# An encoder-decoder block on one core: the two decoder parts under one order, block 0's cross attention among the second batch's units, feed-forward weights loaded in the tail

## The chip, the cores and the metric

The kernel runs on one core of a Trainium2 chip. The metric is the device time of one execution in microseconds (us), as the median of several timed runs. One further execution was recorded by the hardware profiler; all views of the profile come from it. The engines are named as the profile does: PE (TensorE, matmuls and transposes) with PEld (its weight loads), DVE (VectorE), ACT (ScalarE), POOL (GpSimd) and SP (SyncE, which issues the DMAs here). Each engine works through its own instructions in order.

## The reference

Everything is float32, with D = 512, 16 heads of 32, a feed-forward width of 2048, and two batches. The context (2 x 77 x 512) goes through one encoder layer; the target x (2 x 2048 x 512) through one decoder layer that attends to it:

```python
x = src                                              # context, 77 rows per batch
x = x + _mha(_ln(x), _ln(x), enc..., bias=eb)        # encoder self attention
x = x + relu(_ln(x) @ enc_ff1_w.T) @ enc_ff2_w.T
memory = x
y = tgt                                              # 2048 rows per batch
y = y + _mha(yn, yn, dec_sa..., bias=sb)             # yn = _ln(y); sb: relative bias, causal
y = y + _mha(_ln(y), memory, dec_ca..., bias=cb)     # cross attention over 77 keys
y = y + relu(_ln(y) @ dec_ff1_w.T) @ dec_ff2_w.T
```

(Biases and the norms' scales and shifts are left out here; the kernel has them.) The relative bias depends on the distance of key and query, clamped at 127.

## The kernel before

Each batch of 2048 rows is cut into four blocks of 512 (`NMB`), each block into four tiles of 128 rows (`TB`): eight blocks in all, numbered 0 to 7. Every name with a small t is a tile of a block.

**Part one: self attention (and the encoder).** A unit is one tile of 128 queries and one group of four heads: 16 units to a block, 128 in all, and units 64 to 127 are the second batch. A loop over the units writes the order out by hand. For unit n it issues `slot(n)`, and then for each piece of up to four blocks of keys: `turn` (TensorE transposes the probabilities, L365, and DVE or ACT copies them to `pts`, L369 and L371), scores of a later unit (`scores`, L321, with the maximum and copy to `pp` on DVE, L330 and L337, and the exponential on ACT, L345), and `values` (L384). Even units keep their probabilities at the low end of the big buffer `pp`, odd units at the high end, each in four times (block + 1) x 512 columns. `slot(n)` runs what is listed for that unit: `light[n]` (short steps: norms of the next block, the division by the softmax sums in two steps, residual rows, loads of the bias) and then `jobs[n]` (a projection each of queries, keys, values or the output: 4 matmuls of 128x512, L185, L196, L207, L219). A job's weights are loaded two jobs ahead. The encoder is cut into stages, which stand in `light` of the first units; its results, keys and values for the cross attention, go to DRAM (`ckT_d`, `cv_d`). After the last unit, 16 more slots hold the rest: the last division in the first two of them, the output projections of block 7 (L219) seven to ten slots after the last unit. Self attention's results go to DRAM as `y1`, row tile by row tile.

**Part two: cross attention and feed-forward.** It has its own pools of SBUF and PSUM, which take the place of part one's. All its weights are loaded at its beginning (`w_1` and `w_2`, the feed-forward's, with 4 MB each). A block's cross attention (`cross_slots`) is laid over 32 slots: the norm of each tile in three stages (statistics; centering on DVE, L809, with the next bias row added by POOL, L810; transposes, L814, copied by ACT, L819, and DVE, L821), queries (L893), then per tile scores (L833; DVE adds the bias for the first two tiles of a batch, L841, takes the maximum, L843, and subtracts it, L844), exponential, sums and division (POOL, L852), transposes (L860), values (L872), output (L881), and the next norm. A block's feed-forward (`forward_slots`) has 16 first-layer groups (L924) and 16 second-layer quarters (L930), one per slot. The main loop runs block n's feed-forward and block n + 1's cross attention side by side, slot by slot. Block 0's cross attention has no feed-forward beside it and stands alone ahead of the loop:

```python
nT3 = late()
for _ in cross_slots(*steps[0], ys_of[0], nT3):
    pass
for n, (b, m) in enumerate(steps):
    ...
    for _ in range(SLOTS):
        next(side, None)
        next(feed)
```

SyncE issues every DMA in the order in which the program writes it, and waits in that order. In PSUM, part one has seven rotating banks and one (`ot`) for the values' sums; part two has six rotating and two for the feed-forward.

Of the kernel before, what the change touches and what calls it, by code (L numbers as in the profile page):

```python
# [17 lines left out]
P = 128  # L18
# [36 lines left out]
def tile_encoder_decoder(ctx: ExitStack, tc: tile.TileContext, ins, out):  # L55
# [82 lines left out]

    y1 = [
        [dram.tile([P, TB, D], F32, name=f"y1_{b}_{m}", tag=f"y1_{b}_{m}") for m in range(NMB)]  # L140
        for b in range(B)
    ]
    with (
# [10 lines left out]
        END = 2 * HC * T  # L154
        bv = bcast_row(ac, "sa_bv")
        bo = bcast_row(ac, "dec_sa_out_b")
        def bank():
            return ps.tile([P, 512], F32, name="s", tag="s", bufs=7)
# [8 lines left out]
        def small_w(c0):  # L167
            w = sb.tile([P, NC, P], F32, name="wqk", tag="wqk", bufs=3)
            nc.sync.dma_start(w, wchunk("dec_sa_in_wT", c0, P))
            return w  # L170

        def big_w(kind, b, m):
            if wbig.get("is") != (kind, b, m):
                w = sb.tile([P, NC, D], F32, name="wbig", tag="wbig")
                nc.sync.dma_start(
                    w, wchunk("dec_sa_in_wT", 2 * D) if kind == "v" else wchunk("dec_sa_out_wT", 0)
                )
                wbig["is"], wbig["w"] = (kind, b, m), w
            return wbig["w"]
# [73 lines left out]
        def norm_turn(b, m, t):  # L253
            xn = xs.pop((b, m, t))
            if t == 0:
                nTs[b, m] = sb.tile([P, NC, MB], F32, name="nT", tag="nT")
# [94 lines left out]
        def turn(n, j):  # L351
# [9 lines left out]
            for o, group in enumerate(order):  # L361
                pt = bank()
                pts = sb.tile([P, HC, P], F32, name="pts", tag="pts", bufs=6)
# [10 lines left out]
        def values(n, j):  # L374
            b, m, g, t = units[n]
            k0, kn = parts[n][j]
            if t == 0 and j == 0:
                state["ot"] = ps.tile([P, TB, P], F32, name="ot", tag="ot", bufs=1)
# [9 lines left out]
            if t == TB - 1 and j == len(parts[n]) - 1:  # L388
                o = sb.tile([P, TB * P], F32, name="oT", tag="oT", bufs=6)
                nc.scalar.copy(o, ot)  # L390
                ots[b, m, g] = o
# [276 lines left out]

        blocks = [(b, m) for b in range(B) for m in range(NMB)]
# [4 lines left out]
        for x, (b, m) in enumerate(blocks):  # L674
# [14 lines left out]
            for t in range(TB):  # L689
                jobs[u + NU + 7 + t].append(out_job(b, m, t))  # L690
                light[u + NU + 6 + t].append(lambda b=b, m=m, t=t: residual(b, m, t))
# [49 lines left out]

        slot(-1)
# [20 lines left out]
        for n in range(end, end + NU):  # L763
            slot(n)

    with (
        tc.tile_pool(name="bw", bufs=1) as bw,
        tc.tile_pool(name="bsb", bufs=1) as sb,
        tc.tile_pool(name="bsm", bufs=5) as sm,
        tc.tile_pool(name="bps", bufs=1, space=PSUM) as ps,
        tc.manual_schedule(),
    ):
        w_q = bw.tile([P, NC, D], F32, name="w_q")
        w_o = bw.tile([P, NC, D], F32, name="w_o")
        w_1 = bw.tile([P, NC, DFF], F32, name="w_1")  # L780
        w_2 = bw.tile([P, NF, D], F32, name="w_2")
        ckT = bw.tile([P, NC, B * S], F32, name="ckT")
        cv = bw.tile([S, B, D], F32, name="cv")

        cb = [bw.tile([P, H, S], F32, name=f"cb{i}") for i in range(2)]
        SLOTS = NF + TB * NC

        def bank():
            return ps.tile([P, 512], F32, name="s", tag="s", bufs=6)

        def new_y(b, m):
            ys = [sb.tile([P, D], F32, name="y", tag="y", bufs=12) for _ in range(TB)]
            for t, y in enumerate(ys):
                nc.sync.dma_start(y, y1[b][m][:, t, :])
            return ys

        def norm_stages(ys, t, n, row, nT):

            y = ys[t]
            st = sm.tile([P, 6], F32, name="bnst", tag="bnst")  # L800
            mv = sm.tile([P, 2], F32, name="bnmv", tag="bnmv")
            rs = sm.tile([P, 2], F32, name="rstd", tag="rstd")
            nc.vector.bn_stats(st, y)
            nc.vector.bn_aggr(mv, st)
            nc.vector.tensor_scalar_add(rs[:, 0:1], mv[:, 1:2], EPS)
            nc.gpsimd.tensor_tensor(rs[:, 1:2], rs[:, 0:1], mhalf[:, 0:1], ALU.pow)
            yield
            xn = sb.tile([P, D], F32, name="xn", tag="xn", bufs=2)
            nc.vector.tensor_scalar(xn, y, mv[:, 0:1], rs[:, 1:2], ALU.subtract, ALU.mult)  # L809
            nc.gpsimd.tensor_tensor(y, y, row, ALU.add)  # L810
            yield
            pt = bank()
            for c in range(NC):
                nc.tensor.transpose(pt[:, ts(c, P)], xn[:, ts(c, P)], ident)  # L814
            for c in range(NC):
                d = nT()[:, c, ts(t, P)]
                sc, bi = vec(f"dec_{n}_s", c), vec(f"dec_{n}_b", c)
                if c % 2:
                    nc.scalar.activation(d, pt[:, ts(c, P)], AF.Identity, bias=bi, scale=sc)  # L819
                else:  # L820
                    nc.vector.tensor_scalar(d, pt[:, ts(c, P)], sc, bi, ALU.mult, ALU.add)  # L821
            yield

        def attend_stages(b, i, q, y):

            kT, v = ckT[:, :, ts(b, S)], cv[:, b, :]
            pr = sb.tile([P, HC, NC, S], F32, name="pr", tag="pr", bufs=2)
            mx = sm.tile([P, HC, NC], F32, name="mx4", tag="mx4", bufs=3)
            banks = [bank() for _ in range(HC)]
            for g in range(NC):  # L830
                for r in range(HC):
                    rows = slice(r * HD, (r + 1) * HD)
                    nc.tensor.matmul(  # L833
                        banks[r][:, ts(g, S)], q[rows, g, :], kT[rows, g, :], start=True, stop=True
                    )
            for r in range(HC):
                s = banks[r][:, : NC * S].rearrange("p (g k) -> p g k", k=S)
                d = pr[:, r]
                if i < 2:
                    bias = cb[i].rearrange("p (g r) k -> p r g k", r=HC)[:, r]  # L840
                    nc.vector.tensor_tensor(d, s, bias, ALU.add)  # L841
                    s = d
                nc.vector.tensor_reduce(mx[:, r], s, AX.X, ALU.max)  # L843
                nc.vector.tensor_tensor(d, s, mx[:, r, :, None].to_broadcast([P, NC, S]), ALU.subtract)  # L844
            yield
            nc.scalar.activation(pr, pr, AF.Exp)
            yield
            su = sm.tile([P, HC, NC], F32, name="su4", tag="su4", bufs=2)
            ri = sm.tile([P, HC, NC], F32, name="ri4", tag="ri4", bufs=2)
            nc.vector.tensor_reduce(su, pr, AX.X, ALU.add)  # L850
            nc.vector.reciprocal(ri, su)
            nc.gpsimd.tensor_tensor(pr, pr, ri[:, :, :, None].to_broadcast([P, HC, NC, S]), ALU.mult)  # L852
            yield
            yield
            yield
            turned = []
            for g in range(NC):
                pt = bank()
                for r in range(HC):
# [152 lines left out]
```

## Time and profile before

| | us |
|---|---|
| median of 3 runs (lowest, highest) | 3176.05 (3172.75, 3176.2) |
| the profiled execution | 3170.97 |
| its span, from the first to the last instruction | 3169.1 |
| PE busy | 3054.7 (96%) |
| PE weight loads busy | 1732.0 (55%) |
| DVE busy | 1678.5 (53%) |
| ACT busy | 1300.1 (41%) |
| POOL busy | 258.0 (8%) |
| mean granted clock of PE | 0.986 |

A float32 matmul is recorded as two instructions, a transpose as one. In the lists of groups and in timelines, a row gives the start, the length, the engine, the line of the kernel, the operation, the tiles (out<-in), the shape and the count; in brackets stands how long the engine had been idle before and who ended that. Rows of stretches give, for each, the length, each engine's busy time with its instruction count, the granted clock of PE as a share, the busy share of the DMA engines and GB/s. A matmul's end is modelled, so that rows of one line overlap a little.

### The profile page before, as it was taken

What the parts mean: (1) busy time and instruction counts of PE and PEld (TensorE: products, weight loads), DVE (VectorE), ACT (ScalarE), POOL (GpSimd) and SP (SyncE); (2) the same over time, 40 slices, a digit from 0 to 9 for tenths busy, and PEclk for the clock granted to TensorE, in tenths of its full rate; (3) what the DMA queues carried; (4) which work ended last, traced back from release to release, by engine and by line L of the source; (5) the groups of instructions that cost most, each with busy time, mean ns of one, the idle gap of its engine ahead of it and who ended that gap; (6) DMA issues with size and microseconds to landing.
All of it is one profiled execution on the core that took longest, in us unless ns stands there. A gap on an engine that the chain in (4) does not pass through costs nothing. (4 is left out here: it accounts for less than half of the span.)

```text
span 3169.1 us, 56403 instructions
## 1 busy us (share of the span) xinstructions
PE 3054.7 (96%) x22792; PEld 1732.0 (55%) x22792; DVE 1678.5 (53%) x5347; ACT 1300.1 (41%) x2299; POOL 258.0 (8%) x241
## 2 busy tenths in 40 slices
PE   7899999999999999999999858999999999999999
PEld 4565566666665555666666624545454544454544
DVE  4765667666765777676666535434343434343410
ACT  3443466667775555666677702111111111111100
POOL 0100000000000000000000012111111111111100
PEclk9899999999999999999999978999999999999999
DMA  6413201101111312111011070000000000000000
GB/s 154 106 43 117 79 21 48 55 21 38 31 35 58 84 48 62 50 31 35 18 31 48 2 223 1 4 24 4 24 4 24 4 24 4 24 4 10 4 10 13
DMA packets 103860, 128.42 MB, mean 41 GB/s; under 512 B 12058, under 2 KB 62794, under 8 KB 103090
## 3 DMA queue, kind: packets, MB, share of 16 engines
q1 hardware_dynamic: 103602, 124.83, 13.6%
q8 instruction: 181, 2.97, 0.4%
q14 instruction: 77, 0.63, 0.1%
HBM read 105.03 MB, written 19.77 MB: 39 GB/s over the span
## 5 line engine op out<-in xcount | busy, mean ns | idle before, releaser
L330 DVE TENSOR_SCALAR_CACHE_REDUCE pp<-s 128x512 f32<-128x512 f32 (+3 forms) x1024 | 560.7, 590 | 291.9 <-PE s L321 291.9
L345 ACT ACTIVATE pp<-pp,nm 128x128 f32<-128x128 f32 (+15 forms) x512 | 610.6, 1194 | 151.3 <-DVE nm L344 148.5
L371 ACT COPY pts<-s 128x512 f32<-128x512 f32 (+3 forms) x816 | 408.6, 581 | 413.6 <-PE s L365 412.4
L365 PE MATMUL s<-ident,pp 128*128 128x128 f32 x4352 | 544.2, 276 | 13.8 <-ACT pp L345 10.7
L365 PEld LDWEIGHTS s<-ident,pp 128*128 128x128 f32 x4352 | 481.1, 142 | 119.0 <-issue 98.3
L924 PE MATMUL ff<-nT,w 128*128 128x512 f32 x1024 | 457.3, 596 | 0.5 <-DVE nT L821 0.5
L930 PE MATMUL ff<-w,hT 128*128 128x512 f32 x1024 | 454.9, 594 | 0.0
L321 PE MATMUL s<-kT,q 32*128 32x512 f32 (+3 forms) x2560 | 378.9, 575 | 2.3 <-ACT kT L197 0.8
L384 PE MATMUL ot<-pts,vv 128*32 128x128 f32 x8704 | 341.5, 279 | 28.8 <-DVE pts L369 26.5
L384 PEld LDWEIGHTS ot<-pts,vv 128*32 128x32 f32 x8704 | 219.6, 109 | 266.9 <-issue 142.0
L924 PEld LDWEIGHTS ff<-nT,w 128*128 128x128 f32 x1024 | 190.7, 191 | 221.8 <-issue 219.2
L930 PEld LDWEIGHTS ff<-w,hT 128*128 128x128 f32 x1024 | 189.6, 190 | 215.9 <-issue 214.8
L337 DVE CUSTOM_DVE_ANT_0 pp<-s,bias 128x256 f32<-128x256 f32 (+1 forms) x512 | 210.0, 410 | 63.0 <-PE s L321 63.0
L126 ACT ACTIVATE hT<-ff,vecs 128x512 f32<-128x512 f32 x64 | 44.0, 687 | 431.9 <-PE ff L924 431.8
L369 DVE COPY pts<-s 128x512 f32<-128x512 f32 (+3 forms) x328 | 195.6, 644 | 46.7 <-PE s L365 44.9
L321 PEld LDWEIGHTS s<-kT,q 32*128 32x128 f32 x2560 | 135.7, 183 | 76.3 <-issue 47.1
L819 ACT ACTIVATE nT<-s,vecs 128x128 f32<-128x128 f32 x128 | 58.5, 457 | 242.7 <-DVE nT L821 216.7
L865 ACT COPY pts<-s 77x512 f32<-77x512 f32 x64 | 37.2, 581 | 279.3 <-PE s L860 279.3
L821 DVE TENSOR_SCALAR nT<-s,vecs 128x128 f32<-128x128 f32 x128 | 52.4, 409 | 169.8 <-PE s L814 135.9
L128 DVE TENSOR_SCALAR hT<-ff,vecs 128x512 f32<-128x512 f32 x64 | 48.1, 751 | 152.5 <-PE ff L924 152.5
L185 PE MATMUL s<-nT,wqk 128*128 128x512 f32 x256 | 122.9, 625 | 0.5 <-DVE nT L267 0.5
L881 PE MATMUL s<-w_o,oT 128*128 128x512 f32 x256 | 120.5, 615 | 0.7 <-ACT oT L877 0.7
(111 smaller groups left out, 2628.8 us busy)
## 6 DMA issues: line engine op xcount, KB each, us to landing
wqk<-in_dec_sa_in_wT_dram SPq DMA_DIRECT2D x64, 256.0 KB, 3.7
bias<-tz SPq DMA_DIRECT2D x128, 128.0 KB, 3.5
wbig<-in_dec_sa_in_wT_dram SPq DMA_DIRECT2D x8, 1024.0 KB, 8.0
vv<-in_enc_ff_wT_dram SPq DMA_DIRECT2D x8, 1024.0 KB, 5.8
wbig<-in_dec_sa_out_wT_dram SPq DMA_DIRECT2D x8, 1024.0 KB, 7.8
xr<-in_x_dram SPq DMA_DIRECT2D x32, 256.0 KB, 7.4
y<-xr SPq DMA_DIRECT2D x32, 256.0 KB, 2.5
y<-y SPq DMA_DIRECT2D x32, 256.0 KB, 4.4
```

The costliest lines, as they stand in the source:

```text
L185: nc.tensor.matmul(mm, w[:, c, :], nTs[b, m][:, c, :], start=(c == 0), stop=(c == NC - 1))
L321: nc.tensor.matmul(banks[r][:, : kn * P], q[rows4(r), ts(t, P)], kT[rows4(r), g, k0 * P : (k0 + kn) * P], start=True, stop=True,)
L330: nc.vector.tensor_scalar(p[:, k0 * P : (k0 + far) * P], s[:, : far * P], 1.0, None, ALU.mult, ALU.max, accum_out=st["mx"][:, r, c : c + 1],)
L337: nc.vector.tensor_tensor_reduce(p[:, (i + 1) * P - w : (i + 1) * P], s[:, far * P : kn * P], biases[b, m, g][:, r, 2 * P - w :], 1.0, LOW ...
L345: nc.scalar.activation(p[:, : (i + 1) * P], p[:, : (i + 1) * P], AF.Exp, bias=nm, accum_out=sums_of[b, m, g][:, t, r : r + 1],)
L365: nc.tensor.transpose(pt[:, ts(x, P)], p[r][:, ts(k0 + k, P)], ident)
L369: nc.vector.tensor_copy(pts[:, : len(group), :], pt[:, :w])
L371: nc.scalar.copy(pts[:, : len(group), :], pt[:, :w])
L384: nc.tensor.matmul(ot[rows4(r), t, :], vv[:, k0 + k, ts(g * HC + r, HD)], got[r, k], start=(k0 + k == 0), stop=(k0 + k == nb - 1),)
L881: nc.tensor.matmul(mm, oT[:, ts(c, P)], w_o[:, c, :], start=(c == 0), stop=(c == NC - 1))
L924: nc.tensor.matmul(mm, w_1[:, c, ts(f, P)], nT[:, c, :], start=(c == 0), stop=(c == NC - 1))
L930: nc.tensor.matmul(mm, hT[:, f, ts(t, P)], w_2[:, f, :], start=(f == 0), stop=(f == NF - 1))
```

## The change

- The second part's pools go. Both parts run in one schedule, on one set of places: PSUM is one tile of eight banks with a counted rotation; `nTt`, `wbt`, `pts_all`, `oT_all` are fixed tiles. In the second part `w_1` lies in the lower half of `pp`, `w_2` in its upper half, `hT` in `kT`, the residual rows (three blocks' worth) and the normalized rows in `vv`, probabilities in `oT_all`, cross keys in the last two places of `pts_all`.
- Block 0's cross attention is issued in `light` of units 64 to 93 (`first_cross`), with its data in parts of `pp`, `kT` and `vv` that the second batch's first two blocks don't use. Its loads stand in slots 64 and 69. Its results are stored: normalized and transposed rows to `nT3_d`, residual rows back to `y1`, for each tile in slots 84, 87, 90 and 93.
- In slot 123 those normalized rows, one bias row and three of four slices of the cross query weights are loaded; in slot 127 `w_1`, the fourth slice and the cross values. After the last unit come block 1's residual rows and the cross keys, then the softmax division in two steps with a first-layer group of block 0's feed-forward after each, and then block 7's output projections, now two to five slots after the last unit. After these, the cross output weights, a bias row, block 0's residual rows and `w_2` are loaded, and the loop over the blocks follows. In it block 1's cross attention runs beside the 30 slots that are left of block 0's feed-forward.
- The number of matmuls and transposes, and of other engines' operations, stays.

```diff
+        nTt = ac.tile([P, NC, MB], F32, name="nT")
+        wbt = ac.tile([P, NC, D], F32, name="wbig")
+        pts_all = ac.tile([P, 6, HC * P], F32, name="pts")
+        oT_all = ac.tile([P, 6, TB * P], F32, name="oT")
+        psum = ps.tile([P, 8, 512], F32, name="psum")
+        count = {"bank": 0, "banks": 7, "pts": 0, "oT": 0, "mm": 0}
         def bank():
-            return ps.tile([P, 512], F32, name="s", tag="s", bufs=7)
+            i = count["bank"] % count["banks"]
+            count["bank"] += 1
+            return psum[:, i, :]
...
+        def first_cross():
...
+            at(0, loads)
+            at(5, more_loads)
+            for t in range(TB):
+                fs = norm_stages(
+                    y, "n2", rows["dec_ca_out_b"], lambda: xn, lambda t=t: nT[:, :, ts(t, P)]
+                )
+                for k, f in enumerate(fs):
+                    at(1 + t + k, f)
+            for g in range(NC):
+                at(7 + g, lambda g=g: q_group(g, wq[:, :, ts(g, P)], nT, qT[:, g, :]))
+            for t in range(TB):
+                fs = attend_stages(
+                    lambda g, t=t: qT[:, g, ts(t, P)], kTc, vc, y, t < 2, prs[t % 2], pts, lambda: oT, wo
+                )
+                for k, f in zip((0, 1, 2, 4, 5, 6), fs):
+                    at(11 + 3 * t + k, f)
+                fs = norm_stages(y, "n3", rows["dec_ff2_b"], lambda: xn, lambda: slab)
+                for k, f in enumerate(fs):
+                    at(18 + 3 * t + k, f)
+                at(20 + 3 * t, store)
...
-                jobs[u + NU + 7 + t].append(out_job(b, m, t))
-                light[u + NU + 6 + t].append(lambda b=b, m=m, t=t: residual(b, m, t))
+                end = x == len(blocks) - 1
+                jobs[u + NU + (2 if end else 7) + t].append(out_job(b, m, t))
+                at = u + NU + ((-1, 0, 3, 4)[t] if end else 6 + t)
+                light[at].append(lambda b=b, m=m, t=t: residual(b, m, t))
...
+        for r, fs in first_cross().items():
+            light[len(units) // 2 + r] += fs
+        w_1 = pp[:, : END // 2].rearrange("p (c o) -> p c o", c=NC)
+        w_2 = pp[:, END // 2 :].rearrange("p (f o) -> p f o", f=NF)
+        hT = kT.rearrange("p c (f n) -> p (c f) n", n=MB)
...
+        light[len(units) - 5].append(early_loads)
+        light[len(units) - 1].append(w_1_loads)
...
+            def mm_bank():
+                count["mm"] += 1
+                return psum[:, 6 + count["mm"] % 2, :]
...
-        for n in range(end, end + NU):
+        late_loads()
+        feed = feed_forward(0)
+        slot(end)
+        next(feed)
+        slot(end + 1)
+        next(feed)
+        for n in range(end + 2, end + 6):
             slot(n)
+        nc.sync.dma_start(wbt, wchunk("dec_ca_out_wT", 0))
+        row_into(bo, "dec_ff2_b")
+        new_y(0)
+        nc.sync.dma_start(w_2, ins["dec_ff2_wT"].rearrange("(c p) o -> p c o", p=P))
+        count.update(bank=0, banks=6)
+        for x in range(len(blocks)):
+            if x + 2 < len(blocks):
+                new_y(x + 2)
+            if x:
+                feed = feed_forward(x)
+            side = cross(x + 1) if x + 1 < len(blocks) else iter(())
+            done = object()
+            while True:
+                next(side, None)
+                if next(feed, done) is done:
+                    break
+            for _ in side:
+                pass
```

## The prediction

> **What bounds the kernel now.** I read the page's forty slices first (79.2 us each), to see where TensorE is not the bound.
>
> ```profile
> PE   7899999999999999999999858999999999999999
> DVE  4765667666765777676666535434343434343410
> PEclk9899999999999999999999978999999999999999
> ```
>
> TensorE is at nine tenths or more nearly everywhere; the kernel's time is its matmuls plus the places where they wait. Two places stand out: the start, and the stretch around slices 24 to 25, where PE falls to 5 and its clock to 7. That is the join of the two decoder parts. The timeline of TensorE there:
>
> ```profile
> 1820.03 1.97 PE L365 MATMUL s<-ident,pp 128*128 128x128 f32 x16
> ...
> 1824.04 0.63 PE L404 MATMUL s<-ident,rirows 128*128 128x128 f32 x4 [0.29 <-DVE rirows L399]
> 1824.51 13.90 PE L219 MATMUL s<-wbig,oT 128*128 128x512 f32 x32
> 1848.72 1.09 PE L814 MATMUL s<-ident,xn 128*128 128x128 f32 x4 [10.31 <-DVE xn L809]
> 1861.98 1.11 PE L814 MATMUL s<-ident,xn 128*128 128x128 f32 x4 [12.17 <-DVE xn L809]
> ...
> 1950.68 8.75 PE L924 MATMUL ff<-nT,w 128*128 128x512 f32 x16 [0.50 <-DVE nT L821]
> ```
>
> The last output projection of part one (L219) ends at 1838.4, the first feed-forward matmul (L924) starts at 1950.7. Between them stands only the cross attention of block 0, with nothing to fill its waits. Busy time by stretch (length, PE, PEld, DVE, ACT, POOL, then granted clock, DMA share, GB/s):
>
> ```profile
> 980.00:1260.00 280.00, 277.22 (x2312) 162.85 (x2314) 196.74 (x778) 155.25 (x364) 14.38 (x16) 1.00 0.23 65
> ...
> 1838.40:1950.70 112.30, 65.00 (x418) 35.79 (x417) 54.89 (x112) 18.35 (x31) 24.09 (x21) 0.74 0.47 146
> 1950.70:3166.40 1215.70, 1214.70 (x4960) 590.13 (x4960) 420.99 (x833) 177.44 (x290) 163.55 (x141) 1.00 0.04 12
> ```
>
> The middle row is the join: 65 us of 112.3 busy, at 0.74 of the clock. The last is all that follows: TensorE without a gap. The first is units 64 to 93, where the change puts block 0's cross attention: TensorE is full there too (277.2 of 280), so moved matmuls cost their whole length; VectorE has 83 us left.
>
> **The join's gain.** Work on TensorE is conserved: every matmul remains. What block 0's cross attention costs when nothing waits: the last row holds eight feed-forwards and seven crosses in 1214.7 us; the feed-forwards are 2048 matmul records at 0.429 us (32 of L219 in 13.90 give the same), 878.6; the rest by 7 is 47.8 us. (Check: 65.00 x 0.74 = 48.1.) So 112.3 - 47.8 = 64.5 us are waits and half clock. The first two feed-forward groups at 1950.68 take 8.75 where 16 records take 7.03 elsewhere: 1.7 more. Removed: **66.2 us**.
>
> **The tail's new costs.** The first-layer weights (4 MB in 4 DMAs) go into the lower half of pp when unit 127, an odd one, uses the upper. Unit 126's last turn is at 1802.6 to 1804.1, so SyncE gets past that wait at about 1804; the before kernel moved such weights at 387 to 429 GB/s in 10 us stretches, some 10.5 us with 2 to start: there by 1817, needed at 1823.8. SyncE's queue has nothing unmet ahead of them (the stored outputs of units 119 to 122, block 0's normalized rows, a bias row, three weight slices). Behind them stand block 1's rows (waiting for values over vv's blocks 4 to 7, about 1819), the cross keys (for the last pts places, 1823.7) and the remaining residual rows: needed 10 us later or more. Feed-forward group 0 takes the bank of ot and waits for ScalarE's copy of it (0.57 and a signal): **0.8 us**. Two groups of 3.44 us then cover the softmax division, and the output projections follow without a gap. The residuals for t = 2 and 3 chain store, load, POOL add (about 2.5, 2.6, 1.3 us) behind t = 0 and 1; VectorE's add for t = 3 comes about 1 us after its matmul, and what is queued behind it, the bias-relu of group 2, is due 2.7 us later still: nothing. Second-layer weights (4 MB, after the last projection) are wanted 14 groups of 3.44 us and half a cross later: hidden. As groups 0 and 1 have gone ahead, block 1's cross outlasts block 0's feed-forward by two of 32 slots, and block 1's feed-forward waits for the last turn: **0.5 us**, as at 1950.68.
>
> **The second batch's new costs.** TensorE's 47.8 us are in the balance. VectorE gets, by the rows of before: score stages 4 x (0.473 + 0.474 + 0.559) = 6.0 us for each of two biased tiles and 4 x (0.470 + 0.479) = 3.8 for the others, in all 19.6; row sums 6.7; turned copies 5.5; output adds 2.8; eight norms of 2.38, 19.0; queries 3.0: 56.6 us. Its load goes from 196.7 of 280 to 253 of about 340, 75%: it isn't the bound. But it works in order, and a score stage is a burst: behind it stand the pts copies that the same unit's values wait for. In slot 75 (from 1063.2) TensorE reaches its values about 7 us after the score; VectorE has 6.0 of burst, 0.75 of queries and two copies of 0.69: about 2 us late. In slot 78 VectorE is still 3 us behind with unit 79's scores when the slot begins: 3.5 us late. The unbiased tiles meet longer slots (11 us and 4.5 more of moved matmuls): 0.7 each. The norm stages at slots 67 to 70 and the rest: 2. Sum 8.9.
>
> SyncE gets 26 more DMAs here: nine in slot 64 (some 2.5 MB; next weight slice needed at slot 67), nine in slot 69, and eight stores in slots 84 to 93, each waiting for the stage it follows. Behind those stand weight slices and residual rows loaded two jobs ahead: hidden. If a slice came late, about 4 us (its 3.7 from issue to landing). POOL gets 24 us in a stretch where it was busy 14 of 280. The fixed places in PSUM give the old rotation of seven banks and one: nothing.
>
> **The clock.** The nearest row for such stalls is the encoder, put between units of the first batch in the same way:
>
> ```profile
> 110.39 1.95 PE L384 MATMUL ot<-pts,vv 128*32 128x128 f32 x22 [3.35 <-DVE pts L369]
> ...
> 121.38 2.51 PE L384 MATMUL ot<-pts,vv 128*32 128x128 f32 x30 [2.51 <-DVE pts L369]
> ```
>
> ```profile
> 100.00:110.00 10.00, 6.91 (x66) 4.12 (x62) 9.66 (x31) 4.77 (x11) 3.01 (x3) 1.00 0.11 32
> 110.00:120.00 10.00, 7.73 (x84) 5.45 (x84) 8.20 (x26) 4.72 (x13) 0.55 (x1) 0.83 0.84 126
> 120.00:130.00 10.00, 7.61 (x54) 4.02 (x54) 9.06 (x30) 5.06 (x14) 1.16 (x2) 0.72 0.62 164
> ```
>
> Both waits stand behind score bursts of VectorE, and after each the clock falls (0.83, 0.72). The Trainium skill ("TensorE: Matmul & The Clock Gate", What's actually happening) has the clock halve only after an idle window of about 3.4 us. By that rule my stalls, at most 3.5 us, would mostly cost no clock, and the sum is 3120; by the row 2.51 us sufficed. I follow the row: two half-rate windows, each of 3.4 us by that page's estimate, lose 1.7 us: 3.4.
>
> Stalls with clock: 8.9 + 3.4 = **12.3 us**, bounds 3 (VectorE's bursts nearly absorbed) and 31 (each of four score stages loses 6 us and half a window: 4 x 7.7). I take 12 because the encoder's two stalls, 3.35 and 2.51, are of this size.
>
> **Sum.** 66.2 - 0.8 - 0.5 - 12.3 = 52.6 us. The profiled execution took 3170.97 (span 3169.1 and 1.9 around it): 3118.4 for it. The timed median, 3176.05, is 5 us above that execution; on it, **3123 us**.
>
> **Rivals.** (1) *Bursts absorbed.* Stalls of 3 us: 3114. For it: VectorE's share of 70%. Against: the 3.35 us above. (2) *Bursts in full*, 31 us: 3142. For it: the clock after each encoder stall. Against: slots 81 and 84 carry much more matmul work to wait under. (3) *The weights aren't loaded in the tail.* If the wait on pp is met only when unit 127 has turned (1822), they land at about 1834.5; 11 us idle and a slow window: 3135. Against: the two halves belong to different units. (4) *Slower: VectorE becomes the bound of units 64 to 93 and the clock stays low.* From 100 to 160 us, VectorE at 75 to 97% until 150, busy time times clock is 41.2 of 60: 31% lost. The new stretch holds 325 us of matmuls; at that loss it takes 471, 146 lost: 3256. It decides once the stretch loses 17%. For it: the same construction. Against: the encoder met the next block's norms and put all its copies on VectorE; here the load averages 75% and there are four bursts in 30 slots.
>
> **How the numbers follow.** Likeliest case 56% (3113 to 3133), rival 1 11%, rival 2 17%, rival 3 8%, rival 4 6%, and 2% that losses just consume the gain. Within 0.2% is about what a measurement here can't tell from no change. Faster: 92%; same 2%; slower 6%. The range, 3108 to 3144, spans rivals 1 to 3 and drops rival 4.
>
> **What would show it.** Right: the gap before the first feed-forward matmul gone, clock near 1.00 there, that matmul less than 2 us after the last value matmul; units 64 to 93 longer by about 60 us in all; single waits of 2 to 4 us of value matmuls on pts copies in slots 75 and 78. Wrong: the first feed-forward matmul waiting on a DMA; the clock below 0.9 over slots 64 to 93; waits in the tail on SyncE's loads or on bank reuse.

## The result, and the profile after

| | before | after |
|---|---|---|
| median of six runs, us (lowest, highest) | 3172.28 (3168.15, 3176.20) | 3112.98 (3111.87, 3115.81) |
| profiled execution, us | 3170.97 | 3115.81 |
| its span, us | 3169.1 | 3114.0 |
| PE busy | 96% | 98% |
| mean granted clock of PE | 0.986 | 0.993 |

The changed kernel takes 0.9814 of the time before (95% interval 0.9801 to 0.9826): 59.3 us between the medians. Predicted were 3123 us.

The forty slices of the changed kernel (77.9 us each):

```profile
PE   7899999999999999999999989999999999999999
DVE  5665567766765777667666652434242434342410
PEclk9899999999999999999999999999999999999999
```

The hole of slices 24 and 25 is gone, and so is the fall of the clock there. What the join became is seen in TensorE's timeline of the changed kernel (start, length, what; in brackets the idle time before and who ended it):

```profile
1878.71 0.42 PE L406 MATMUL psum<-pts,vv 128*32 128x128 f32 x8 [0.17 <-DVE pts L391]
1879.84 3.70 PE L1002 MATMUL psum<-nT,pp 128*128 128x512 f32 x8 [0.70 <-ACT oT L412]
1883.38 0.60 PE L426 MATMUL psum<-ident,rirows 128*128 128x128 f32 x4
1884.98 3.70 PE L1002 MATMUL psum<-nT,pp 128*128 128x512 f32 x8 [1.00 <-DVE oT L427]
1888.52 13.90 PE L241 MATMUL psum<-wbig,oT 128*128 128x512 f32 x32
```

The last values matmul (L406) ends at 1879.1, the first feed-forward group (L1002) starts at 1879.8. Before, 112 us lay between the last projection and the first feed-forward matmul. Its weights (the first of the four loads was issued at 1845.5, earlier than forecast) are there. Two waits for a PSUM bank stay, 0.70 and 1.00 us. Busy time by stretch in the changed kernel (length, PE, PEld, DVE, ACT, POOL, then clock, DMA share, GB/s):

```profile
980.00:1313.60 333.60, 328.25 (x2733) 194.49 (x2733) 247.87 (x890) 172.70 (x395) 38.24 (x36) 1.00 0.28 75
```

```profile
1878.70:1902.30 23.60, 21.89 (x61) 9.85 (x62) 3.96 (x7) 1.27 (x2) 3.08 (x3) 1.00 0.20 66
1902.30:3111.30 1209.00, 1207.29 (x4945) 588.62 (x4943) 420.53 (x832) 173.56 (x287) 164.27 (x141) 1.00 0.06 19
```

The first row is the second batch with the cross attention in it: VectorE 247.87 of 333.60, 74%, and the clock at 1.00. The second is the join, the third all that follows.

The trace gives a ledger: between the starts of the same matmuls in both profiled executions ("turn" is a unit's first transpose), in us:

| stretch | before | after | difference |
|---|---|---|---|
| span's start to unit 0's turn | 45.5 | 44.1 | -1.4 |
| unit 0 to unit 16 (the encoder among them) | 152.4 | 153.2 | +0.8 |
| unit 16 to unit 64 | 792.4 | 793.7 | +1.3 |
| unit 64 to unit 96 (the cross attention put in) | 292.8 | 346.3 | +53.5 |
| unit 96 to unit 127's last turn | 538.6 | 539.8 | +1.2 |
| from there to the third feed-forward group of block 0 | 138.0 | 25.1 | -112.9 |
| from there to the last matmul | 1205.1 | 1207.4 | +2.3 |

The sum is -55.2, within 0.1 the difference of the spans. The rest of the medians' 59.3 is run to run: the profiled execution of the changed kernel is the longest of its six, the one of before lies 1.3 us under its median.

In the row of +53.5, 47.8 us are the moved matmuls, so 5.6 are stalls. As idle time TensorE shows only 2.6 of them (5.5 us in this stretch, 2.9 before); where the rest is hidden is shown with the experiments. In the row of -112.9, the same 47.8 are work that left, so 65.1 are waits and half clock that went.

### The profile page after: what moved, and what is told of

It is laid out like the page before. It is cut to its first block, busy times and chain, and to the rows that moved or that the text cites. A ratio compares the mean times of both kernels' runs of the same rounds, so it can differ in the third digit from the quotient of the medians.

```text
span 3114.0 us, 55824 instructions
## 1 busy us (share of the span) xinstructions
PE 3042.2 (98%) x22792; PEld 1728.7 (56%) x22792; DVE 1674.3 (54%) x5347; ACT 1295.9 (42%) x2299; POOL 258.6 (8%) x241
## 5 line engine op out<-in xcount | busy, mean ns | idle before, releaser
L352 DVE TENSOR_SCALAR_CACHE_REDUCE pp<-psum 128x512 f32<-128x512 f32 (+3 forms) x1024 | 560.5, 589 | 292.1 <-PE psum L343 292.1
L393 ACT COPY pts<-psum 128x512 f32<-128x512 f32 (+3 forms) x816 | 408.4, 581 | 431.3 <-PE psum L387 422.5
L387 PE MATMUL psum<-ident,pp 128*128 128x128 f32 x4352 | 545.7, 276 | 13.7 <-ACT pp L367 11.4
L387 PEld LDWEIGHTS psum<-ident,pp 128*128 128x128 f32 x4352 | 482.2, 142 | 119.3 <-issue 97.6
L1002 PE MATMUL psum<-nT,pp 128*128 128x512 f32 x1024 | 455.8, 595 | 2.4 <-DVE oT L427 1.0
L1008 PE MATMUL psum<-pp,kT 128*128 128x512 f32 x1024 | 457.3, 596 | 0.0
L343 PE MATMUL psum<-kT,q 32*128 32x512 f32 (+3 forms) x2560 | 383.6, 580 | 3.3 <-ACT kT L219 0.8
L406 PE MATMUL psum<-pts,vv 128*32 128x128 f32 x8704 | 342.0, 280 | 30.5 <-DVE pts L391 28.0
L406 PEld LDWEIGHTS psum<-pts,vv 128*32 128x32 f32 x8704 | 219.9, 110 | 270.6 <-issue 146.4
L1002 PEld LDWEIGHTS psum<-nT,pp 128*128 128x128 f32 x1024 | 189.9, 190 | 222.5 <-issue 217.6
L343 PEld LDWEIGHTS psum<-kT,q 32*128 32x128 f32 x2560 | 135.5, 184 | 80.8 <-issue 45.6
L207 PE MATMUL psum<-nT,wqk 128*128 128x512 f32 x256 | 122.3, 622 | 0.5 <-DVE nT L289 0.5
L218 PE MATMUL psum<-nT,wqk 128*128 128x512 f32 x256 | 117.5, 602 | 0.1
```

Of the source, the lines that this page charges most:

```text
L207: nc.tensor.matmul(mm, w[:, c, :], nTs[b, m][:, c, :], start=(c == 0), stop=(c == NC - 1))
L218: nc.tensor.matmul(mm, w[:, c, :], nTs[b, m][:, c, :], start=(c == 0), stop=(c == NC - 1))
L343: nc.tensor.matmul(banks[r][:, : kn * P], q[rows4(r), ts(t, P)], kT[rows4(r), g, k0 * P : (k0 + kn) * P], start=True, stop=True,)
L352: nc.vector.tensor_scalar(p[:, k0 * P : (k0 + far) * P], s[:, : far * P], 1.0, None, ALU.mult, ALU.max, accum_out=st["mx"][:, r, c : c + 1],)
L387: nc.tensor.transpose(pt[:, ts(x, P)], p[r][:, ts(k0 + k, P)], ident)
L393: nc.scalar.copy(pts[:, : len(group), :], pt[:, :w])
```

## The experiments

My theory: the gain comes from the move; what it costs in the second batch is VectorE's bursts in front of TensorE; the tail's waits are small. The rivals are with each run. Where a time is compared with the changed kernel's, that is 3112.98. "Unit 64 to 96" is the stretch of the ledger, read from each run's own trace.

### Block 0's cross attention back at the join, on the new places

The rest of the change stays: one schedule, fixed places, the first-layer weights in the tail.

```diff
-        for r, fs in first_cross().items():
-            light[len(units) // 2 + r] += fs
+        first = first_cross()
...
-        slot(end)
-        next(feed)
-        slot(end + 1)
-        next(feed)
-        for n in range(end + 2, end + 6):
+        for n in range(end, end + 6):
             slot(n)
+        for r in sorted(first):
+            for f in first[r]:
+                f()
+        late_loads()
+        feed = feed_forward(0)
```

(Its rows lie in `vv` and the upper half of `pp`, and its normalized rows go to `nTt` without DRAM.)

> Block 0's cross attention stands alone again between part one's last projection and the loop, on the fixed places, with first-layer weights still loaded in slot 127 and no early feed-forward groups. My theory (the gain is the waits and the half clock of that join, 66 us less what the insertion loses): the time goes back to that of the kernel before, 3172 us, within 8 either way, the clock at the join falls to about 0.75, and units 64 to 96 last 47.8 + 5.2 = 53 us less than in the changed kernel. Rival (part of the gain comes from the fixed places or from the early loads): the time stays 20 us or more under the kernel before.

3161.6 us, 0.997 (0.996 to 0.998) of before: 48.6 over the changed kernel and some 10 under before. Unit 64 to 96 is back at 293.6. From the last turn to the third group it took 127.7 us, against 138.0 before. The join in this run, by stretch and then by TensorE's waits:

```profile
1839.00:1940.00 101.00, 64.63 (x419) 35.92 (x420) 54.39 (x112) 19.24 (x32) 23.40 (x20) 0.78 0.24 66
```

```profile
1845.33 1.12 PE L714 MATMUL psum<-ident,kT 128*128 128x128 f32 x4 [8.12 <-DVE kT L708]
1849.65 1.12 PE L714 MATMUL psum<-ident,kT 128*128 128x128 f32 x4 [3.20 <-DVE kT L708]
...
1886.26 3.48 PE L767 MATMUL psum<-ident,pp 128*77 128x128 f32 x16 [9.64 <-POOL pp L761]
```

The same 65 us of PE as before, again at under 0.8 of the clock: alone at the join, the cross attention is a chain of waits whatever its places. But the first two waits are 8.12 and 3.20 where before had 10.31 and 12.17. Neither expectation held for the time: by far the larger part of the gain is the move, but some 10 us are the rest of the change. I read them as the order of loads. The traces bear that out for the second wait, 9.0 of the 10. POOL's addition of a bias row, before and then in this run:

```profile
1859.57 1.26 POOL L810 TENSOR_TENSOR y<-y,row_dec_ca_out_b 128x512 f32<-128x512 f32 x1 [11.64 <-DMA row_dec_ca_out_b<-in_rows_dram]
```

```profile
1847.24 1.26 POOL L709 TENSOR_TENSOR vv<-vv,kT 128x512 f32<-128x512 f32 x1 [2.55 <-DMA kT<-in_rows_dram]
```

Before, SyncE issued that row at 1845.9, behind 1 MB of query weights; here at 1840.9, ahead of them. POOL's part of the second tile's norm stands behind the addition, VectorE's centering (L809) behind that, and TensorE's transposes last. That the order alone gives the 10 us was not tried by itself.

### The tail: groups after the projections, and other banks

The first run puts the two early feed-forward groups behind the projections; the second leaves them early, but swaps their two PSUM banks and restarts the rotation.

```diff
         slot(end)
-        next(feed)
         slot(end + 1)
-        next(feed)
```

> The two first feed-forward groups run after the projections of block 7 instead of covering the division; all else as in the changed kernel. My theory (conserved work; what counts is the waits): the waits of 0.70 and 1.00 us ahead of the two groups and the 0.67 us at block 1's feed-forward go, a wait of about 0.3 us on the division comes: 2 us faster than the changed kernel, so 3111. Rival (the groups cover the division, and without them the projections wait for it): 2 to 4 us slower, 3116.

```diff
-                return psum[:, 6 + count["mm"] % 2, :]
+                return psum[:, 7 - count["mm"] % 2, :]
...
         feed = feed_forward(0)
+        count.update(bank=0)
         slot(end)
```

> The early groups take bank 6 and then bank 7 (ot), and the rotation is set back to bank 0 ahead of them, so that neither the copy of ot nor the division's transposes stand in their way. My theory: the waits of 0.70 and 1.00 us ahead of the two groups fall under 0.3 each; 1.4 us faster than the changed kernel, 3111.5. Rival (the second wait is the product with the sums itself and not its bank): only the first wait goes, 0.7 us.

3112.63 (0.9816, 0.9801 to 0.983) and 3111.83 (0.9816, 0.9801 to 0.9831). Neither differs from the changed kernel by what runs can tell. Timeline of TensorE in the run with the banks swapped:

```profile
1877.55 3.70 PE L1002 MATMUL psum<-nT,pp 128*128 128x512 f32 x8
1881.09 0.60 PE L426 MATMUL psum<-ident,rirows 128*128 128x128 f32 x4
1881.53 3.60 PE L1002 MATMUL psum<-nT,pp 128*128 128x512 f32 x8
```

No bracket is left: the 0.70 and 1.00 were waits for banks, the second for the bank of the division's broadcast (L426), which `ot`'s bank alone doesn't explain. With the groups behind the projections, the division waits only 0.20 us for its rows: the early groups cover nothing of weight.

The medians can't tell, but the stretch from unit 127's last turn to the last matmul can, since no half rate falls in it. It took 1232.6 us in the changed kernel and, within 0.1, in four more executions whose tail is the same (without the bias, two slots, and the first run of each encoder edit). With the groups behind the projections it took 1229.8, with the banks swapped 1230.5. The expectations had 2 and 1.4 us less; the traces show 2.8 and 2.1.

### The weights after the projections

```diff
-        light[len(units) - 1].append(w_1_loads)
...
         slot(end)
-        next(feed)
         slot(end + 1)
-        next(feed)
         for n in range(end + 2, end + 6):
             slot(n)
+        w_1_loads()
```

> First-layer weights, the last query slice and the cross values are loaded after block 7's projections, and no groups go ahead. My theory: SyncE reaches these loads behind the store of the last residual row, some 6 us after TensorE's last projection; the first of four 1 MB loads lands 5 us later; TensorE waits about 12 us, one half-rate window follows (1.7): 14 us slower than the changed kernel, 3127. Rival (only the first of the four loads counts and block 1's norm fills the wait): 3 to 6 us slower, 3118.

3120.76 us (0.9843, 0.9828 to 0.9858): 7.8 over the changed kernel. TensorE in this run:

```profile
1898.14 9.35 PE L1001 MATMUL psum<-nT,pp 128*128 128x512 f32 x16 [8.66 <-DMA pp<-in_dec_ff_wT_dram]
```

One wait on the DMA, as expected, and the first matmuls behind it at half rate (16 take 9.35, not 7.03). But it is 8.66 us where my theory had about 12, and the cost of 7.8 us lies between its 14 and the rival's 3 to 6. Each load of 1 MB serves four groups, and no wait follows for the other three.

### What the cross attention costs where it now is

Three runs of one execution each. The first leaves out block 0's cross attention proper (scores to output; norms, queries and stores stay), the second leaves out its relative bias, and the third puts the four tiles two slots apart instead of three.

```diff
-                for k, f in zip((0, 1, 2, 4, 5, 6), fs):
-                    at(11 + 3 * t + k, f)
```

> Leaves out block 0's cross attention itself (scores, exponential, sums, turns, values, output projection); its norms and queries stay in units 64 to 93. From unit 64's first turn to unit 96's the changed kernel took 346.3 us, the kernel before 292.8. TensorE loses 4 x (1.07 + 1.83 + 1.00 + 3.44) = 29.4 us of matmuls. My theory (the rest of the insertion's price stands behind the two biased score bursts of VectorE, 1.5 and 3.3 us): 312 us. Rival (the price comes from the norms, the stores and SyncE's loads): 317.

```diff
-                    lambda g, t=t: qT[:, g, ts(t, P)], kTc, vc, y, t < 2, prs[t % 2], pts, lambda: oT, wo
+                    lambda g, t=t: qT[:, g, ts(t, P)], kTc, vc, y, False, prs[t % 2], pts, lambda: oT, wo
```

> Leaves the relative bias out of block 0's cross attention, which shortens the score burst of its first two tiles on VectorE from 6.0 to 3.8 us; matmuls stay. My theory (TensorE's next scores wait for banks that the burst still holds): the stalls at slots 75 and 78 fall from 1.5 and 3.3 us to 0 and 1.1, so 342.6 us from unit 64 to unit 96 instead of 346.3. Rival (VectorE's whole load sets it): 346.3 less 0.5.

```diff
-                    at(11 + 3 * t + k, f)
+                    at(11 + 2 * t + k, f)
...
-                    at(18 + 3 * t + k, f)
+                    at(18 + 2 * t + k, f)
...
-                at(20 + 3 * t, store)
+                at(20 + 2 * t, store)
```

> Block 0's four score stages stand two slots apart instead of three (slots 75, 77, 79, 81). My theory (each burst costs by what VectorE still has to do at that slot, and the short units of the first block have no room for more): the stalls grow by 3 us to 349.5 from unit 64 to unit 96, 3 more if the clock falls. Rival (the room is an average over the stretch): 346.3 as before.

Unit 64 to 96, us: 292.8 before, 313.4 without the attention, 342.7 without the bias, 346.3 changed, 357.4 with two slots. The times were 3078.76, 3105.35 and 3123.89.

Without the attention it is close to my 312, without the bias on my 342.6. Without the bias 49.9 us are added for 47.8 of matmuls: 2.1 us of stall. So of the 5.6, the bias of two tiles makes 3.6. TensorE's waits in unit 78 (the cross scores of the second biased tile stand at 1103.3), for the same eight matmuls before and in the changed kernel:

```profile
1087.72 0.93 PE L321 MATMUL s<-kT,q 32*128 32x384 f32 x8
```

```profile
1109.58 0.91 PE L343 MATMUL psum<-kT,q 32*128 32x384 f32 x2
1110.99 0.91 PE L343 MATMUL psum<-kT,q 32*128 32x384 f32 x2 [0.51 <-DVE pp L748]
1112.61 0.91 PE L343 MATMUL psum<-kT,q 32*128 32x384 f32 x4 [0.72 <-DVE vv L232]
```

The wait isn't where I put it. The values find their copies in time; it is the next unit's scores (L343) that wait for banks which VectorE has yet to empty, with the cross attention's bias addition (L748) and a values projection's output (L232). The brackets hold 1.2 us, but the stall is 3.0. Before, the four heads' matmuls ran side by side, and the next work began 0.86 us after the first of them; now they come in twos, each pair about as long as all eight were, and it begins after 3.88. A TensorE that is busy with one head counts as busy. Over the stretch this line's busy time grew from 57.4 to 61.5 us with the same 400 matmuls. With the tiles two slots apart:

```profile
1102.19 0.44 PE L387 MATMUL psum<-ident,pp 128*128 128x128 f32 x2 [1.71 <-DVE pp L748]
1103.60 1.12 PE L343 MATMUL psum<-kT,q 32*128 32x512 f32 x2 [0.97 <-DVE pp L748]
1106.64 2.07 PE L343 MATMUL psum<-kT,q 32*128 32x512 f32 x4 [0.50 <-DVE vv L232]
```

3.2 us within 6, and the clock fell for 6.8 us at once, and again for 6.8 at 1252.8 behind two waits of 0.57 and 0.42. This cost 11.1 us in the stretch, where my theory had 3.2, or 6 with the clock. At the 1.5 to 1.8 us that 3.4 us of half rate cost (below), the clock makes 6 to 7 of them and stalls the other 4 to 5, in this one execution.

### Tiles one slot later

The three later tiles move one slot on, into longer slots; the early groups stand behind the projections.

```diff
-                    at(11 + 3 * t + k, f)
+                    at(11 + 3 * t + (t > 0) + k, f)
```

(The norms and stores move with it.)

> Tiles 1 to 3 of block 0's cross attention start one slot later (79, 82, 85), and the two early feed-forward groups run after the projections. My theory: in slot 79 the burst meets 2.5 us of work left on VectorE, not 3.5, and 4 us more of matmuls ahead of the next scores: the stall of 3.3 us falls to 1, so 344 us from unit 64 to unit 96, and 3110 us in all. Rival (the turns of tile 0, which now share that slot, take the room): 346.

3108.96 us, but with an interval of 0.9762 to 0.9852 that can't tell it from the changed kernel. Unit 64 to 96 took 346.4, which reads as the rival's number; but this execution had a window of half rate of 3.4 us at 1120.9, and one such window cost 1.7 us elsewhere (below). Without it, 344.7, near my 344. One execution can't settle it.

### When does the clock fall?

My forecast took a fall of the clock from the encoder, where the same construction stalls. It came in one of these runs and not in another, so I used all profiled executions that run the second batch unchanged: the changed kernel, the three edits of the tail, and four more whose edit is in the encoder (next section). In all eight the waits are alike, 0.51 and 0.72 us of idle time within 2.5 us. Unit 64 to 96 took 346.3 or 346.4 in five of them, with no half rate; 347.9 and 348.1 in two, with one stretch of 3.4 us at half rate; and 349.3 in one (weights after the projections), with 6.8 us. So 3.4 us at half rate cost 1.5 to 1.8 us, where the forecast had 1.7.

All half-rate stretches of an execution, but for one cut off by its end, are whole multiples of 3.413 us and begin on one grid of that step, and its phase differs between executions. The Trainium skill has that ("TensorE: Matmul & The Clock Gate", What's actually happening: the activity window is free-running); but where it has the clock halve after an idle window, here a window that was idle for about a quarter was enough. On this grid, the windows around the two waits. The changed kernel (columns as above; PE busy is the first number after the length, the clock the third from the end):

```profile
1108.04:1111.45 3.41, 2.90 (x17) 1.82 (x15) 3.23 (x8) 0.96 (x2) 0.00 (x0) 1.00 0.70 172
1111.45:1114.87 3.42, 2.70 (x35) 1.52 (x34) 3.39 (x11) 0.00 (x0) 0.00 (x0) 1.00 0.00 0
1114.87:1118.28 3.41, 3.41 (x19) 2.21 (x18) 1.90 (x6) 2.29 (x3) 0.00 (x0) 1.00 0.01 2
```

The run with the weights after the projections:

```profile
1103.96:1107.38 3.42, 2.53 (x11) 1.07 (x9) 3.28 (x8) 0.79 (x2) 0.00 (x0) 1.00 0.41 107
1107.38:1110.79 3.41, 3.08 (x29) 1.56 (x29) 3.11 (x11) 0.00 (x0) 0.00 (x0) 0.50 0.00 0
1110.79:1114.20 3.41, 3.41 (x18) 3.41 (x17) 0.69 (x1) 1.17 (x3) 0.00 (x0) 0.50 0.01 2
```

In the first, the boundary falls between the two waits: 0.5 us idle in one window and 0.72 in the next, and the clock stays. In the second, 0.9 us fall into one window, and the next is at half rate. The other six go the same way: idle times of 0.5 and 0.72 in the four that kept the clock, 0.97 and 1.06 in one window in the two that lost it. So it is the same stall, and the outcome goes with the phase of the grid. Two limits: idle time alone isn't the rule, for elsewhere in these traces windows with 1.0 to 1.5 us of idle kept the clock, and a few, most of them in the encoder, lost it with 0.3 to 0.6 (0.47 with the tiles one slot later); and that the phase is the cause is an agreement in eight executions, not something I could set.

### Why the encoder stalls more

The prediction's nearest row was the encoder, which no part of the change touches: 3.35 and 2.50 us of waits, 27.3 us at half rate. If it is the way its bursts are cut, the second batch escapes by its own cut, and the encoder could be mended. First edit: the two batches' score stages a slot further apart.

```diff
+            yield lambda: exp(0)
+
             def stage():
-                exp(0)
                 score(1)
-
-            yield stage
-
-            def stage():
                 normalize(0)
-                exp(1)
 
             yield stage
+            yield lambda: exp(1)
             yield lambda: normalize(1)
             yield lambda: turn_p(0)
```

> The changed kernel with one edit in the encoder, which the change left as it was: the second batch's score stage no longer stands in one slot with the first one's exponential (it goes to the next slot, with the first one's normalization, and its own exponential one further). Same work. The question is why the clock fell in the encoder and not in the second batch. Theory: waits of 2.5 to 3.4 us in one piece behind two score bursts close together bring the half rate, shorter and separate ones do not. Then the waits of 3.35 and 2.50 us in value matmuls near 109 and 120 us fall to below 1.5 us each, the half-rate windows between 100 and 155 us shrink from 27.3 us to at most 10, units 0 to 16 take about 146 us instead of 149 to 154, and the time is about 3108. Rival, that the clock falls there because the encoder keeps VectorE at nine tenths for 50 us, whatever stands where: the waits only move, 20 us or more at half rate stay, units 0 to 16 take 149 to 154 us, and the time stays at 3113.

> The changed kernel with the encoder's score stages apart and, in the tail, the two PSUM banks of the feed-forward swapped and the rotation restarted, so that its first two groups do not wait. Same work. It tells whether the two edits together beat the changed kernel by more than a run-to-run difference. Theory: 0.70 and 1.00 us of waits in the tail go as they did alone, and the encoder gives 3 to 6 us: 3107 (3104 to 3111), units 0 to 16 in 145 to 148 us, as in the run with the encoder's edit alone. Rival, that neither is more than noise: 3111 to 3115, units 0 to 16 at 149 us or more.

The second of these runs also has the tail's banks swapped. In both, part of the computation differs from the reference: the encoder is one slot longer, and by the program's order the values of block 1 are written over part of its output weights before the second batch's projection reads them. Engines, instructions and sizes are the same, so the times can be read. They were 3111.25 (0.981, 0.9793 to 0.9826) and 3109.59 (0.9805, 0.979 to 0.982). The premise was wrong: the wait of 3.35 us stayed, with the first score stage alone, and the 2.50 moved a slot on. 23.9 and 17.1 us at half rate remained between 100 and 155; units 0 to 16 took 147.8 and 147.0, between the two expectations, but units 16 to 64 took 795.3 and 794.8, where the changed kernel took 793.7.

Second edit: VectorE's score stage (1.63 us of bias, 1.43 of maximum, 1.44 of subtraction in one piece) is cut in two slots, with the number of slots kept.

```diff
-                nc.vector.tensor_reduce(mx[:S], pr, AX.X, ALU.max)
-                nc.vector.tensor_tensor(
-                    pr, pr, mx[:S, :, :, None].to_broadcast([S, HC, NC, S]), ALU.subtract
-                )
 
             def exp(b):
+                pr = pra[b].rearrange("p (r g k) -> p r g k", r=HC, g=NC)
+                mx = sm.tile([P, HC, NC], F32, name="emx", tag="emx", bufs=2)
+                nc.vector.tensor_reduce(mx[:S], pr, AX.X, ALU.max)
+                nc.vector.tensor_tensor(
+                    pr, pr, mx[:S, :, :, None].to_broadcast([S, HC, NC, S]), ALU.subtract
+                )
                 nc.scalar.activation(pra[b], pra[b], AF.Exp)
```

(The stages follow as in the first edit, but `normalize(1)` and `turn_p(0)` share a slot.)

> The changed kernel with the encoder's score stage cut in two on VectorE: the bias add (1.63 us) stays in its slot, maximum and subtraction (1.43 and 1.44 us) go to the next slot, ahead of the exponential; the second batch's score stage moves one slot on, and the encoder keeps its number of slots. Same work. In the changed kernel VectorE had 1.5 us of a norm, 4.5 us of the score stage and 0.7 us of bias strips in one piece ahead of the copies for which TensorE waited 3.35 us. Theory: it is the length of one burst ahead of the copies that makes the encoder's waits, and the cross attention in the second batch is spared because its score stage is four short pieces: the waits of 3.35 and 2.50 us fall to 1.5 us or less, half rate between 100 and 155 us falls from 27.3 us to at most 10, units 0 to 16 take 141 to 145 us, the time is 3101 to 3107. Rival, that VectorE's load of nine tenths there makes the waits, however it is cut: they turn up in other slots, 17 us or more stay at half rate, units 0 to 16 take 147 to 154 us, and the time is 3109 to 3115.

> The same edit of the encoder, and in the tail the feed-forward's two PSUM banks swapped and the rotation restarted, so that its first two groups do not wait. Same work. A second look at the encoder's stretch, and whether the two together beat the changed kernel by more than runs differ. Theory: units 0 to 16 in 141 to 145 us again, the tail's waits of 0.70 and 1.00 us gone, 3099 to 3106. Rival: units 0 to 16 in 147 to 154 us, 3108 to 3114.

3114.42 (0.9824, 0.9808 to 0.9841) and 3112.11 (0.9817, 0.9803 to 0.9832): no gain. TensorE's waits in the first of these two runs:

```profile
108.56 1.31 PE L406 MATMUL psum<-pts,vv 128*32 128x128 f32 x22 [1.35 <-DVE pts L391]
117.92 1.21 PE L343 MATMUL psum<-kT,q 32*128 32x256 f32 x2 [4.82 <-ACT pts L393]
...
138.04 2.07 PE L343 MATMUL psum<-kT,q 32*128 32x512 f32 x2 [3.17 <-ACT pts L393]
```

and the stretch in that run, then in the changed kernel:

```profile
95.00:160.00 65.00, 54.02 (x462) 34.65 (x461) 50.85 (x178) 30.23 (x83) 8.60 (x7) 0.82 0.38 91
```

```profile
95.00:160.00 65.00, 56.15 (x458) 35.77 (x457) 50.08 (x177) 30.00 (x83) 8.61 (x7) 0.79 0.37 87
```

The 3.35 became 1.35, as the cut would have it, and 4.82 and 3.17 turned up elsewhere: 23.9 and 20.5 us at half rate, units 0 to 16 in 151.7 and 151.8 us. The rival holds: cutting the score stage only moves the waits. The new waits end on ScalarE's copies, but these stand behind the encoder's exponential (L542), which waits for VectorE's subtraction:

```profile
116.17 1.23 ACT L542 ACTIVATE pp<-pp 77x1232 f32<-77x1232 f32 x1 [3.81 <-DVE pp L539]
```

It is the same ahead of the 3.17 (there the exponential waits 2.81). Of the two explanations, VectorE's load (50 of 65 us) is the one left, and it fits; no run lowers that load, so it is not shown.

No version here beats the changed kernel's median by more than runs differ.

## Why the prediction was right, and where it was off

**The join's gain.** Right. 66.2 less 0.8 were forecast for this place; the ledger shows 65.1. The working "matmuls are conserved, all else in 112.3 us goes" held. What it didn't see is that the 65 us have two causes: with the cross attention back at the join, the other edits still gave some 10 us.

**The tail.** Weights in time: right, and with more room than forecast, since the first of four loads is enough for four groups. That sharpens rival 3: loaded later still, after the projections, they cost 7.8 us, not its price. The wait for `ot`'s bank was 0.70 against 0.8; the second group's 1.00 us for the division's bank was not forecast. Block 1's feed-forward waits 0.67 where 0.5 was said, but its stretch of the ledger grew by 2.3. With the two groups behind the projections that stretch took 1206.1 us, not 1207.4: the early groups are 1.4 of the 2.3, the wait among them. Nearly all of the other 0.9 is in the norms' transposes, start to start: the same 220 took 25.2 us before and 26.0 in that run. Why is open.

**The second batch.** That VectorE's bursts hold TensorE up was right; the path, and with it the size, was off. The step said 8.9 us of stalls plus 3.4 of clock; it measured 5.6 and 0 in the profiled execution. By term, from unit to unit in the trace: slot 75, 2 forecast, 1.5 measured; slot 78, 3.5 and 3.1; the two unbiased tiles, 1.4 and nothing; norms at slots 66 to 70, 2 and 2.2. The measured ones make 6.8, not 5.6, mainly because the moved matmuls took 46.9 us here (from start to start, idle time left out), not 47.8. The waits fell on scores and their banks, not on values and `pts`; so the nearness of 3.1 to 3.5 is luck. The load of VectorE was right: 75% forecast, 74% measured.

**The clock.** The choice between row and rule was half right. The row said that waits well under 3.4 us can halve the clock, and they can: a stall of 3 us, with 1.2 us of idle time, did so in three of eight executions. But the row was taken as a certainty, where it is a matter of phase here: two windows were forecast, and none, one or two came. The step that failed is "two half-rate windows: 3.4"; over the eight executions the mean is (1.7 + 1.8 + 3.0) / 8, some 0.8 us. And the encoder was a poor row for the size: VectorE there is loaded as the second batch never is.

**The sum.** 52.6 us forecast, 55.2 between the profiled executions: stalls and clock came 6.7 smaller, the rest (1.8 more than forecast after the join, 1.2 before it, 0.7 up to unit 64, 0.3 at the join) took 4.0 back. That they offset each other in part is luck. Two of its rows are the clock's. With the encoder unedited, units 16 to 64 took 792.4 us in the executions with one half-rate stretch there (3.4 us), that of before among them, and 793.7 or 793.8 in those with two, the changed kernel's among them. From unit 96 to the last turn the changed kernel's execution has 10.2 us at half rate; three others of the same instructions there, with 3.4, took 537.5 to 537.7 us, not 539.8. These two rows differ between executions and are no price of the change. The remaining 4 us to the medians' 59.3, and 3.8 between the 3176.05 that the forecast stood on and the median of six runs, are the spread of runs. A part of it has a place: units 0 to 16, which no part of the change touches, took 148.8 to 153.6 us in the profiled executions with the encoder unedited.

Of the rivals, *bursts absorbed* (3114) named the time best, with 3 us of stall against 5.6 measured; 3113 is the lower edge of the likeliest case. *Bursts in full* would have wanted more than five times the stall. *VectorE becomes the bound* failed at its premise: it takes over the encoder's loss, where VectorE was at 82 to 97% in the rows shown; here it was at 74%.

## What to carry to other kernels

Work that stalls when it stands alone, because nothing fills its waits, can be cut into stages and put between units of a full TensorE: here it then cost its matmuls and 12% more. Most of the price here (3.6 of 5.6 us) went when VectorE's score stages were shorter by the bias, and the waits shown were for PSUM banks that VectorE had yet to empty. So leave slots between the stages (three slots cost 5.6 us; two cost 11 more in one execution, about half of it by the clock). To price an edit of a few us, compare a stretch that has no half rate in either trace: it told 2 us apart here, where the medians could not. When a forecast needs a stall's size, take it from a stretch with the same load on the engine that stalls, not from one built in the same way.

## What the runs showed of the hardware

Half rate on TensorE came in windows of 3.413 us on a grid whose phase differs from run to run, and in eight executions two waits of 0.51 and 0.72 us cost no clock where the grid's boundary fell between them (five), and 1.6 to 3.0 us where it did not (three). That makes a difference of 3 us between two single executions of the same stretch no evidence of anything: compare the stretch's clock first.
